# Separate TensorE allowances for preparation and layer 1, and the norm behind layer 1's attention as a thread of its own

## The chip, the cores and the metric

The kernel runs on one core of a Trainium2 chip. The metric is the device time of one execution in microseconds (us); lower is better. Executions of one kernel scatter by about 0.3% here, so kernels are compared by several runs taken on the same chip in the same rounds. The record marks every timed run below as fast (none is over 1.5% above the fastest of the same kernel), so fast runs are compared with fast ones.

## The reference, cut to what matters

Eight images of 256 channels and 32x32 pixels go through two layers in float32. Layer 0 has eight heads that attend from 1024 pixels to 1426 pooled keys. Layer 1 is one full attention over an image's 1024 tokens, followed by eight experts that every token visits.

```python
# layer 0: keys and values from four pooled sizes with a depthwise convolution
attn = softmax(einsum('bhqd,bhkd->bhqk', q_g, k) * SCALE)      # 1024 x 1426 per head
x = x + proj(einsum('bhqk,bhkd->bhqd', attn, v) ...)
# layer 1
t = to_tokens(x)
t = t + attention(_ln_t(t))                                    # 1024 x 1024, one head of 256
t = t + experts(_ln_t(t))                                      # 8 experts, two hidden layers, one output
```

The gates of the experts need the mean over all images, so the last expert products can only start when layer 1's attention is done for the last image. Until then the first two products of some experts are computed and their result is parked in HBM ("staged").

## The kernel before

A scheduler at build time (`Flow`) fixes the order of every engine's instructions. The main loop emits layer 0's attention in 384 steps: four score matmuls, one exponential on ScalarE, four value matmuls of the step before. Between the steps it resumes threads of other work, as long as an allowance of TensorE time lasts. A thread says before each piece on which engine it will run and which tiles it needs.

```python
PACE = 3.2
CAP = 1.5

    def runnable(self, need):
        engine, tiles, tag = need
        ...
        if engine == "PE":
            until = max(pe, self.free("sc") - 0.5)        # when the scores' buffer comes free
            slot = self.free(tag) if tag is not None else 0.0
            return (not self.closed
                and (self.credit > 0 or pe < until - 0.5) # allowance left, or TensorE idle anyway
                and at + MARGIN <= until and slot <= until)
        ...
    def resume(self, thread):
        ...
        self.credit -= self.now["PE"] - pe                # what the piece took
    def step(self, pace=None):
        ...
            self.credit = min(self.credit + pace, CAP * pace)
        while True:
            thread = next((t for t in self.threads if self.runnable(t[1])), None)
```

Threads are kept by rank: queries 0, projection 1, keys and values 2, preparation of the next image 4, layer 1's outputs 5, layer 1's scores 6, the convolution on VectorE 7. The output of layer 1 for one quarter of an image, with its norm inline:

```python
        def outputs():
            for i in range(4 * nb):
                ...
                res = T(l1, [P, 2, C], "res")
                f.sp.dma_start(res, t1[b][:, :, q])
                ...                                        # sums, reciprocal, 16 matmuls into ps
                o = T(l1, [P, 2, C], "o")
                f.ve.tensor_tensor(o, ps, rec, ALU.mult)
                for m in range(2):
                    f.ve.scalar_tensor_tensor(o[:, m, :], o[:, m, :], gb[:, m : m + 1], res[:, m, :], ALU.add, ALU.add)
                f.sp.dma_start(t2[b][:, :, q], o)
                yield from scale_tokens(o, C)              # the norm
                f.sp.dma_start(hn[b][:, :, q], o)
```

Two further places matter below. The projection of layer 0 adds the residual from one tile, `xr`, which is loaded, added to and stored four times for an image. The exponentials are summed in pairs by accumulating transfers, which GpSimd issues in its own program order, between the operations that pool the next image.

```python
    xt = T(work, [P, 512], "xr")
    f.sp.dma_start(xt, x[b, m * P : (m + 1) * P, sl])
    yield pe(atts[b, 0], atts[b, 1], tag="sm")
    ps = small()                                           # matmuls into a small PSUM buffer
    yield ve(ps, xt)
    f.ve.scalar_tensor_tensor(xt, ps, bias[:, m : m + 1], xt, ALU.add, ALU.add)
```

Of the kernel before, what the change touches and what calls it, by code (L numbers as in the profile page):

```python
# [11 lines left out]
ALU = mybir.AluOpType  # L12
# [4 lines left out]
P = 128  # L17
C = 256
HW = 1024
HEADS = 8  # L20
DH = 32
# [4 lines left out]
NE = 8  # L26
SCALE0 = DH ** -0.5
SCALE1 = C ** -0.5
PACE = 3.2
CAP = 1.5  # L30
NEVER = 1e9
MARGIN = 1.5
AHEAD = {"DVE": 4.0, "ACT": 2.0, "POOL": 4.0, "SP": 10.0}
# [2 lines left out]
PACE2 = 8.0  # L36
# [617 lines left out]
class Flow:  # L654
# [18 lines left out]
    def __init__(self, tc, kit):  # L673
        nc = tc.nc
        self.tc, self.kit = tc, kit
        self.now = dict.fromkeys(("PE", "DVE", "ACT", "POOL", "SP"), 0.0)
        self.last = {}
        self.ready, self.read, self.writer, self.reader, self.slots, self.open = {}, {}, {}, {}, {}, set()
        self.pe = self.Engine(self, "PE", nc.tensor)
        self.ve = self.Engine(self, "DVE", nc.vector)  # L680
        self.act = self.Engine(self, "ACT", nc.scalar)
        self.pool = self.Engine(self, "POOL", nc.gpsimd)
        self.sp = self.Engine(self, "SP", nc.sync)
        self.threads = []
        self.cut = {}
        self.also = {}
        self.credit, self.port = 0.0, 0.0

    def tile(self, pool, shape, tag, bufs=1):
        t = self.kit.tile(pool, shape, tag, bufs=bufs)  # L690
# [111 lines left out]
            self.threads.insert(at, thread)  # L802
        return thread

    def runnable(self, need):
        engine, tiles, tag = need
        if engine is None:
            return tiles()
        at = max([self.ready.get(n, 0.0) for t in tiles for n in self.keys(t)], default=0.0)
        pe = self.now["PE"]  # L810
        if engine == "PE":

            until = max(pe, self.free("sc") - 0.5)
            slot = self.free(tag) if tag is not None else 0.0
            return (
                not self.closed
                and (self.credit > 0 or pe < until - 0.5)
                and at + MARGIN <= until
                and slot <= until
            )  # L820

        now = self.now[engine]
        return now <= pe + AHEAD[engine] if at <= now + 0.3 else at <= pe + NEAR[engine]

    def resume(self, thread):
        pe = self.now["PE"]
        thread[1] = next(thread[0], None)
        if thread[1] is None:
            self.threads = [t for t in self.threads if t is not thread]
        self.credit -= self.now["PE"] - pe  # L830

    def step(self, pace=None):


        self.closed = pace is None
        if pace is not None:
            self.credit = min(self.credit + pace, CAP * pace)
        while True:
            thread = next((t for t in self.threads if self.runnable(t[1])), None)
            if thread is None:  # L840
                return
            self.resume(thread)

    def finish(self, done):

        while not done():
            self.credit, self.closed = 1.0, False
            thread = next((t for t in self.threads if t[1][0] is None and self.runnable(t[1])), None)
            self.resume(thread or min((t for t in self.threads if self.possible(t[1])), key=self.start))

# [11 lines left out]
def attention(tc, kit, f, outer, ended, nb, consts, x, t1, t2, hn, bounds, vecs, q_t, kv_t, proj_t, gqk_t, wqk, wqkv, vecs1, w1_d, w1c, gate_d, wrc, vecs2, bnvec):  # L862
# [6 lines left out]
    with ExitStack() as ctx:  # L869
        l1, shared = outer  # L870
# [4 lines left out]
        def T(pool, shape, tag, bufs=1):  # L875
            return f.tile(pool, shape, tag, bufs=bufs)
# [31 lines left out]
        pjw = weight(proj_t, "v", 256, l1)  # L908
        con = kit.con
        ident, grp = kit.ident, con[:, K_GRP : K_GRP + P]  # L910
        heads = T(l1, [P, P + DH], "o")
        nc.scalar.dma_start(heads, consts[:, K_HEAD:K_SEL])
        head = heads[:, :P]

# [692 lines left out]
        def outputs():  # L1607

            for i in range(4 * nb):
                yield until(lambda: len(probabilities) > i)  # L1610
                b, q, p1, v = probabilities[i]
                res = T(l1, [P, 2, C], "res")
                f.sp.dma_start(res, t1[b][:, :, q])
                s = T(l1, [P, 2, C], "s")
                yield ve(*p1[:2])
                f.ve.tensor_tensor(s, p1[0], p1[1], ALU.add)
                for g in range(2, 4):
                    yield ve(p1[g])
                    f.ve.tensor_tensor(s, s, p1[g], ALU.add)
                f.ve.tensor_tensor(s[:, 0, :], s[:, 0, :], s[:, 1, :], ALU.add)  # L1620
                yield pe(s, tag="sm")
                ps = small()
                f.pe.matmul(ps[:, :C], lhsT=kit.ones, rhs=s[:, 0, :], start=True, stop=True)
                yield ve(ps)
                rec = T(l1, [P, C], "rec1")
                n = 8 * (i // 4) + 4 + i % 4
                f.act.activation(ps[:, C:], ps[:, :C], AF.Copy, accum_out=hi[:, n : n + 1])
                f.ve.reciprocal(rec, ps[:, :C])
                f.act.activation(ps[:, C:], rec, AF.Copy, accum_out=lo[:, n : n + 1])
                yield pe(*p1, v, tag="sm")  # L1630
                ps = small()
                for m in range(2):
                    for kc in range(8):
                        if kc % 4 == 0 and (m or kc):
                            yield pe()
                        f.pe.matmul(
                            ps[:, m * C : (m + 1) * C],
                            lhsT=v[:, kc, m * P : (m + 1) * P],
                            rhs=p1[kc // 2][:, kc % 2, :],
                            start=kc == 0,  # L1640
                            stop=kc == 7,
                        )
                taken[0] += 1
                yield ve(ps, rec)
                o = T(l1, [P, 2, C], "o")
                f.ve.tensor_tensor(
                    o, ps.rearrange("p (m q) -> p m q", m=2), rec[:, None, :].to_broadcast([P, 2, C]), ALU.mult
                )
                for m in range(2):
                    f.ve.scalar_tensor_tensor(o[:, m, :], o[:, m, :], gb[:, m : m + 1], res[:, m, :], ALU.add, ALU.add)  # L1650
                f.sp.dma_start(t2[b][:, :, q], o)
                yield from scale_tokens(o, C)
                f.sp.dma_start(hn[b][:, :, q], o)
                written[0] += 1
                ended[0] = written[0] // 4

        def centred(cm, src, width, dst):

# [14 lines left out]
        def weights1():  # L1673
# [15 lines left out]
            ps = small()  # L1689
# [20 lines left out]
            ps = small()  # L1710
# [28 lines left out]
                f.ve.tensor_tensor(c, c, be_, ALU.add)  # L1739

            for e in range(NE):
                we = T(l1, [P, 2, C], "res")
                f.sp.dma_start(we, w1_d[:, e])
                yield act(we)
                wc = T(l1, [P, 2, C], "o")
                yield from centred(cm, we, C, wc)
                f.sp.dma_start(w1c[:, e], wc)
            wr = T(wp, [P, 2, NE], "wr")
# [30 lines left out]
        for i in range(len(steps) + 1):  # L1779
            if i < len(steps):  # L1780
                b, c, half, kc = steps[i]
                sl = slice(half * 512, half * 512 + 512)
                if kc % 4 == 0:
                    f.finish(lambda: key_parts[0] > 3 * b + kc // 4)
                if (half, kc) == (0, 0):
                    f.finish(lambda: (b, c) in qs)
                    turn[0] = 2 * b + c
                    atts[b, c] = T(work, [P, HW], "att", bufs=2)
                pts[i] = scores(b, c, sl, kc)
                f.step()  # L1790
            if i:
                b1, c1, half1, kc1 = steps[i - 1]
                if kc1 == 0:
                    pv = T(psum, [P, 512], "pv")
                    pairs = []
                    sl1 = slice(half1 * 512, half1 * 512 + 512)
                    f.spawn(unit(b1, c1, sl1, i // NKC, pairs), 0)
                f.finish(lambda: kc1 // 4 in vts[b1])
                values(b1, c1, kc1, pts[i - 1], pv)
                if kc1 % 2:  # L1800
                    add(kc1, pts.pop(i - 1), pts[i - 2])
                    pairs.append(pts.pop(i - 2))
                if kc1 == NKC - 1:
                    f.finish(lambda: projected[0] >= b1)
                    f.act.activation(atts[b1, c1][:, sl1], pv, AF.Copy)
            if i < len(steps):
                f.step(PACE)
        f.finish(lambda: projected[0] == nb)
        f.also.clear()
        f.finish(lambda: f.free("sx") < NEVER)  # L1810
# [138 lines left out]
def experts(tc, kit, nb, t2, hn, h2d, w1c, w2_d, wo_d, bnvec, bo_d, gate_d, wrc, consts8, out, f, outer, ended, early):  # L1949
# [11 lines left out]
    with ExitStack() as ctx:  # L1961
# [152 lines left out]
        while not gated and n2 < NSTAGED:  # L2114
            first(n1)
            n1 += 1
            f.step(PACE2)
            if n1 > 1:
                for _ in second(n2, True):
                    pass  # L2120
                n2 += 1
                f.step(PACE2)
        f.finish(lambda: gated)
        early.close()
        wp3 = ctx.enter_context(tc.tile_pool(name="w3", bufs=1, side="right"))
# [309 lines left out]
```

## Time and profile before

| | before |
|---|---|
| time, median of 6 runs (range) | 3496.1 us (3487.3 to 3504.5) |
| profiled span | 3505.2 us |
| TensorE busy | 3237.3 us |
| TensorE idle | 267.9 us, of it 191.2 in layer 0's attention |
| layer 0's attention (first to last exponential) | 106.8 to 2100.7 us |
| first matmul of the experts / first final expert product | 2134.4 / 2405.0 us |

The profile shows for each engine the time in which it had an instruction in work. A matmul that runs at half clock counts as busy, for twice as long: four records of one kind that take 1.88 us elsewhere take 3.78 us behind a gap shown below. This turns out to matter. The prediction below quotes the lines of before; in a line by stretch the columns are the stretch, its length, the busy time of TensorE, its weight loads, VectorE, ScalarE and GpSimd (instructions in brackets), the granted TensorE clock, the DMA share and GB/s.

### The profile page before, as it was taken

What the parts mean: (1) busy time and instruction counts of PE and PEld (TensorE: products, weight loads), DVE (VectorE), ACT (ScalarE), POOL (GpSimd) and SP (SyncE); (2) the same over time, 40 slices, a digit from 0 to 9 for tenths busy, and PEclk for the clock granted to TensorE, in tenths of its full rate; (3) what the DMA queues carried; (4) which work ended last, traced back from release to release, by engine and by line L of the source; (5) the groups of instructions that cost most, each with busy time, mean ns of one, the idle gap of its engine ahead of it and who ended that gap; (6) DMA issues with size and microseconds to landing.
All of it is one profiled execution on the core that took longest, in us unless ns stands there. A gap on an engine that the chain in (4) does not pass through costs nothing.

```text
span 3505.2 us, 39918 instructions
## 1 busy us (share of the span) xinstructions
PE 3237.3 (92%) x15276; PEld 1790.8 (51%) x15276; DVE 2278.6 (65%) x3922; ACT 1676.3 (48%) x2195; POOL 489.1 (14%) x616
## 2 busy tenths in 40 slices
PE   7787899899989989989999997998999999999998
PEld 3322244344424434433544354745777777777776
DVE  6686888778878787685554443314776656666665
ACT  3565766556566565555564542332223333333332
POOL 2122122131131221321121110004000000000000
PEclk9798999999999999999999999999999999999999
DMA  1356655645655564554555556223440000000000
GB/s 47 75 107 152 134 127 111 144 108 111 148 105 110 134 136 109 119 124 111 112 125 136 128 105 219 79 79 107 150 150 19 19 18 24 31 18 19 19 12 20
DMA packets 103880, 333.28 MB, mean 95 GB/s; under 512 B 12848, under 2 KB 38200, under 8 KB 80448
## 3 DMA queue, kind: packets, MB, share of 16 engines
q0 software_dynamic: 24576, 172.51, 25.1%
q1 hardware_dynamic: 75744, 156.16, 13.0%
q8 instruction: 122, 2.00, 0.2%
q10 hardware_dynamic: 3360, 1.97, 0.2%
q14 instruction: 78, 0.64, 0.1%
HBM read 96.23 MB, written 61.87 MB: 45 GB/s over the span
## 4 chain that ended last, share of the span: by engine, by line
PE 53%; DMA 3%; DVE 3%; ACT 2%; issue 1%; POOL 0%; SPq 0%; DVEq 0%; ACTq 0%; POOLq 0%
PE bank L667 24%; PE y L667 11%; PE sm L667 9%; PE sc L667 3%; PE sx L667 3%; PE pv L667 3%; ACT pt L667 2%; DMA pt<-pt 1%; DMA t<-xr 1%; DVE acc L667 1%; DVE rec L667 1%; DMA t<-t 0%; DMA hn<-hn 0%; DMA xr<-in_x_dram 0%; DVE t L667 0%
## 5 line engine op out<-in xcount | busy, mean ns | idle before, releaser
L667 ACT ACTIVATE pt<-sc 128x2048 f32<-128x2048 f32 (+1 forms) x384 | 720.5, 1876 | 358.5 <-PE sc L667 263.0
L667 PE MATMUL sc<-q,kn 32*128 32x512 f32 (+1 forms) x3072 | 460.8, 671 | 134.1 <-ACT pt L667 132.7
L667 DVE SCALAR_TENSOR_TENSOR acc<-p,vec,acc 128x225 f32<-128x225 f32 (+7 forms) x928 | 521.1, 568 | 34.0 <-ACT acc L667 9.3
L667 PE MATMUL bank<-h,w2e 128*128 128x512 f32 x1024 | 481.2, 596 | 0.0
L667 ACT ACTIVATE h<-bank,bnvec 128x512 f32<-128x512 f32 x298 | 229.7, 771 | 480.0 <-PE bank L667 480.0
L667 DVE TENSOR_TENSOR pt<-pt,pt 128x1024 f32<-128x1024 f32 x320 | 383.8, 1242 | 104.7 <-DMA pt<-pt 100.0
L667 PE MATMUL pv<-pt,vt 128*32 128x512 f32 (+1 forms) x3072 | 429.5, 632 | 2.1 <-ACT att L667 2.1
L667 ACT ACTIVATE h<-c,bnvec 128x512 f32<-128x512 f32 x214 | 162.5, 807 | 322.9 <-DVE c L667 322.9
L667 POOL DMA_DIRECT2D pt<-pt x192 | 169.2, 881 | 994.7 <-ACT pt L667 872.4
L667 PEld LDWEIGHTS sc<-q,kn 32*128 32x128 f32 (+1 forms) x3072 | 119.8, 184 | 339.6 <-ACT pt L667 232.4
L667 DVE TENSOR_TENSOR c<-p1c,bank 128x512 f32<-128x512 f32 x107 | 73.6, 688 | 316.9 <-PE bank L667 316.9
L667 PEld LDWEIGHTS bank<-h,w2e 128*128 128x128 f32 x1024 | 194.8, 191 | 151.7 <-issue 139.9
L667 PEld LDWEIGHTS pv<-pt,vt 128*32 128x32 f32 (+1 forms) x3072 | 61.3, 109 | 315.3 <-issue 296.5
L667 POOL TENSOR_TENSOR rstd<-rstd,mhalf 128x4 f32<-128x4 f32 (+2 forms) x88 | 108.8, 1237 | 735.4 <-DVE rstd L667 602.0
L667 DVE TENSOR_TENSOR h<-h,gates 128x1024 f32<-128x1024 f32 x128 | 156.9, 1226 | 71.5 <-DMA h<-h 64.4
L667 PE MATMUL bank<-hn,w1e 128*128 128x256 f32 (+1 forms) x596 | 189.9, 447 | 10.5 <-DMA w2e<-in_w_dram 10.5
L667 PE MATMUL y<-t,s3e 128*128 128x256 f32 x768 | 187.5, 380 | 0.0
L667 PE MATMUL sm<-y,t 128*128 128x256 f32 x736 | 173.2, 383 | 0.0
L667 ACT ACTIVATE p<-sm 128x512 f32<-128x512 f32 (+1 forms) x151 | 88.2, 584 | 169.6 <-PE sm L667 143.5
L667 PEld LDWEIGHTS bank<-hn,w1e 128*128 128x128 f32 x596 | 114.0, 192 | 100.4 <-issue 92.7
L667 DVE RECIPROCAL rec<-rec 128x512 f32<-128x512 f32 x32 | 107.3, 3352 | 89.1 <-ACT rec L667 89.0
L667 PE MATMUL bank<-t,s1e 128*128 128x256 f32 x642 | 156.1, 379 | 2.9 <-DVE t L667 2.9
(291 smaller groups left out, 4679.2 us busy)
## 6 DMA issues: line engine op xcount, KB each, us to landing
pt<-pt POOLq DMA_DIRECT2D x160, 1024.0 KB, 7.4
h<-h SPq DMA_DIRECT2D x72, 512.0 KB, 4.0
xi<-in_x_dram SPq DMA_DIRECT2D x16, 512.0 KB, 7.2
t<-t SPq DMA_DIRECT2D x8, 1024.0 KB, 5.8
res<-t SPq DMA_DIRECT2D x32, 256.0 KB, 6.0
t<-o SPq DMA_DIRECT2D x32, 256.0 KB, 2.8
hn<-o SPq DMA_DIRECT2D x32, 256.0 KB, 5.6
hn<-hn SPq DMA_DIRECT2D x16, 512.0 KB, 5.3
```

The lines of the kernel that those rows point to most:

```text
L667: ins = fn(*args, **kwargs)
```

## The change

The one allowance becomes two. Threads of rank 0 to 4 (the attention's own side work and the next image's preparation) get 4.0 us for each step, threads of rank 5 and up (layer 1) get 2.0 us, each with a carry-over of 1.5 steps. The norm behind layer 1's attention becomes a thread, so that the next quarter's output need not wait for it. To make room, the multiplication by the reciprocal writes PSUM in place, the sum goes into the residual's tile, and that tile gets a second buffer while tile `o` goes.

```diff
-PACE = 3.2
-CAP = 1.5
+FILLER = 5
+PACE = 4.0
+PACE1 = 2.0
+CAP = (1.5, 1.5)
...
-                and (self.credit > 0 or pe < until - 0.5)
+                and (self.credit[rank >= FILLER] > 0 or pe < until - 0.5)
...
-        self.credit -= self.now["PE"] - pe
+        self.credit[thread[2] >= FILLER] -= self.now["PE"] - pe
...
-            self.credit = min(self.credit + pace, CAP * pace)
+            for i in range(2):
+                self.credit[i] = min(self.credit[i] + pace[i], CAP[i] * pace[i])
...
-                res = T(l1, [P, 2, C], "res")
+                yield until(lambda: scaled[0] >= i - 1)
+                res = T(l1, [P, 2, C], "res", bufs=2)
...
-                o = T(l1, [P, 2, C], "o")
-                f.ve.tensor_tensor(o, ps..., rec..., ALU.mult)
+                m2 = ps.rearrange("p (m q) -> p m q", m=2)
+                f.ve.tensor_tensor(m2, m2, rec..., ALU.mult)
                 for m in range(2):
-                    f.ve.scalar_tensor_tensor(o[:, m, :], o[:, m, :], gb..., res[:, m, :], ALU.add, ALU.add)
-                f.sp.dma_start(t2[b][:, :, q], o)
-                yield from scale_tokens(o, C)
-                f.sp.dma_start(hn[b][:, :, q], o)
-                written[0] += 1
+                    f.ve.scalar_tensor_tensor(res[:, m, :], m2[:, m, :], gb..., res[:, m, :], ALU.add, ALU.add)
+                f.sp.dma_start(t2[b][:, :, q], res)
+                f.spawn(norm(b, q, res), 5)
+        def norm(b, q, o):
+            yield from scale_tokens(o, C)
+            f.sp.dma_start(hn[b][:, :, q], o)
+            scaled[0] += 1
+            written[0] += 1
...
-                f.step(PACE)
+                f.step((PACE, PACE1))
```

More of the change, by code (lines that the diff above doesn't have):

```diff
@@ L686, in __init__ @@
         self.also = {}
-        self.credit, self.port = 0.0, 0.0
+        self.credit, self.port = [0.0, 0.0], 0.0
     def tile(self, pool, shape, tag, bufs=1):
@@ L803, in spawn, with runnable @@
         return thread
-    def runnable(self, need):
+    def runnable(self, need, rank=0):
         engine, tiles, tag = need
@@ L836, in step @@
         if pace is not None:
-            self.credit = min(self.credit + pace, CAP * pace)
+            for i in range(2):
+                self.credit[i] = min(self.credit[i] + pace[i], CAP[i] * pace[i])
         while True:
-            thread = next((t for t in self.threads if self.runnable(t[1])), None)
+            thread = next((t for t in self.threads if self.runnable(t[1], t[2])), None)
             if thread is None:
@@ L846, in finish @@
         while not done():
-            self.credit, self.closed = 1.0, False
+            self.credit, self.closed = [1.0, 1.0], False
             thread = next((t for t in self.threads if t[1][0] is None and self.runnable(t[1])), None)
@@ L910, in attention @@
         ident, grp = kit.ident, con[:, K_GRP : K_GRP + P]
-        heads = T(l1, [P, P + DH], "o")
+        heads = T(l1, [P, P + DH], "res", bufs=2)
         nc.scalar.dma_start(heads, consts[:, K_HEAD:K_SEL])
@@ L1644, in outputs @@
                 yield ve(ps, rec)
-                o = T(l1, [P, 2, C], "o")
-                f.ve.tensor_tensor(
-                    o, ps.rearrange("p (m q) -> p m q", m=2), rec[:, None, :].to_broadcast([P, 2, C]), ALU.mult
-                )
+                m2 = ps.rearrange("p (m q) -> p m q", m=2)
+                f.ve.tensor_tensor(m2, m2, rec[:, None, :].to_broadcast([P, 2, C]), ALU.mult)
                 for m in range(2):
-                    f.ve.scalar_tensor_tensor(o[:, m, :], o[:, m, :], gb[:, m : m + 1], res[:, m, :], ALU.add, ALU.add)
-                f.sp.dma_start(t2[b][:, :, q], o)
-                yield from scale_tokens(o, C)
-                f.sp.dma_start(hn[b][:, :, q], o)
-                written[0] += 1
-                ended[0] = written[0] // 4
+                    f.ve.scalar_tensor_tensor(res[:, m, :], m2[:, m, :], gb[:, m : m + 1], res[:, m, :], ALU.add, ALU.add)
+                f.sp.dma_start(t2[b][:, :, q], res)
+                f.spawn(norm(b, q, res), 5)
+        scaled = [0]
+        def norm(b, q, o):
[3 more added lines that the diff above has]
+            written[0] += 1
+            ended[0] = written[0] // 4
         def centred(cm, src, width, dst):
@@ L1741, in weights1 @@
             for e in range(NE):
-                we = T(l1, [P, 2, C], "res")
+                we = T(l1, [P, 2, C], "res", bufs=2)
                 f.sp.dma_start(we, w1_d[:, e])
                 yield act(we)
-                wc = T(l1, [P, 2, C], "o")
+                wc = T(l1, [P, 2, C], "res", bufs=2)
                 yield from centred(cm, we, C, wc)
@@ L2116, in experts @@
             n1 += 1
-            f.step(PACE2)
+            f.step((PACE2, PACE2))
             if n1 > 1:
@@ L2121, in experts @@
                 n2 += 1
-                f.step(PACE2)
+                f.step((PACE2, PACE2))
         f.finish(lambda: gated)
```

## The prediction

> **What bounds the kernel now.** I read the page's slices first, then the busy time of each engine by stretch, then the waits of TensorE, then the instructions in order of time at two places. The slices (tenths busy, 40 slices of 87.6 us):
>
> ```profile
> PE   7787899899989989989999997998999999999998
> DVE  6686888778878787685554443314776656666665
> PEclk9798999999999999999999999999999999999999
> ```
>
> TensorE is at 7 to 9 tenths through slice 24 and nearly full after it; VectorE, at 6 to 8 in the first half, never is. A full TensorE cannot gain from a reordering, so only its idle time counts. The stretches are the four groups of images of layer 0's attention, the start of the tail, the rest of the tail (layer 1 of the last image beside staged expert work), and the experts proper. First column the length, second TensorE busy, the third from the end the granted clock:
>
> ```profile
> 106.80:459.40 352.60, 282.22 (x1595) 101.34 (x1597) 263.50 (x514) 217.45 (x255) 71.71 (x83) 0.90 0.56 124
> 459.40:1032.80 573.40, 523.95 (x2902) 234.56 (x2898) 455.29 (x822) 349.22 (x430) 142.31 (x169) 0.96 0.55 123
> 1032.80:1607.80 575.00, 531.61 (x2926) 243.21 (x2930) 457.64 (x807) 345.89 (x423) 120.04 (x145) 0.97 0.54 120
> 1607.80:2100.70 492.90, 464.94 (x2643) 228.79 (x2637) 255.85 (x397) 268.41 (x297) 71.20 (x82) 0.98 0.54 120
> 2100.70:2200.00 99.30, 79.85 (x248) 43.37 (x247) 38.15 (x60) 23.43 (x38) 7.75 (x8) 0.91 0.60 206
> 2200.00:2404.00 204.00, 197.45 (x616) 111.61 (x614) 39.61 (x79) 74.71 (x117) 14.81 (x31) 0.98 0.21 78
> 2404.00:3505.00 1101.00, 1083.53 (x4156) 790.63 (x4156) 699.36 (x1083) 354.31 (x553) 27.71 (x42) 0.99 0.13 45
> ```
>
> Idle TensorE, length less busy: 70.4 + 49.4 + 43.4 + 28.0 = 191 us in the attention, 19.5 and 6.6 in the tail, 17.5 in the experts. The attention's share of it is what this change can reach. The waits of TensorE in 106 to 2101 us (us in total, times, longest):
>
> ```profile
> PE sc L667 <- ACT pt L667: 132.7, 96, 7.6
> PE sm L667 <- DVE xr L667: 23.7, 6, 5.9
> PE sx L667 <- DMA res<-in_w_dram: 7.3, 1, 7.3
> ```
>
> So 132.7 of the 191 us are scores that wait for the exponential of the step before. Two steps in order of time show the loop:
>
> ```profile
> 1003.16 1.14 PE L667 MATMUL sc<-q,kn 32*128 32x512 f32 x8 [0.65 <-ACT pt L667]
> ...
> 1004.23 1.06 PE L667 MATMUL pv<-pt,vt 128*32 128x512 f32 x8
> ...
> 1004.41 1.88 ACT L667 ACTIVATE pt<-sc 128x2048 f32<-128x2048 f32 x1 [1.31 <-PE sc L667]
> ...
> 1006.35 1.14 PE L667 MATMUL sc<-q,kn 32*128 32x512 f32 x8 [1.05 <-ACT pt L667]
> ```
>
> A step cannot be shorter than 1006.35 - 1003.16 = 3.19 us: scores 1.14, exponential 1.88, handovers. TensorE's own work in it is 1.14 + 1.06 = 2.2 us. So a step with less than 1.0 us of filler (preparation of the next image, or layer 1) leaves TensorE idle, and a step with more is bound by TensorE. That is the lever of this scheduler, and the allowances set how much filler goes into each step.
>
> **What the Trainium skill says.** "PSUM — Partial Sum Buffer", Specifications: 8 banks of 512 FP32 values in each partition. The program takes all eight (scores 4, two small, one spare small, one for the values), so the scores have one buffer; the trace agrees, each score group waiting for the exponential that empties it. "Perfetto Trace Analysis", Identifying Performance Opportunities: repeated gaps can mean too little PSUM for the next tile; here the 96 waits on one tile are that. "TensorE: Matmul & The Clock Gate", Part 2, Step-by-step: matmuls stay in program order. The trace agrees: an expert matmul that waits 10.46 us for its weights (below) holds up layer 1's work behind it. The same page, What's actually happening: after an idle window of about 3.4 us the clock is halved; the trace agrees, since those eight records took 5.92 us, and the next eight of the same kind 3.60.
>
> **The change, part by part.** I compared the instruction order of the two built programs.
>
> *Removed or added work: none on TensorE.* Every kind of matmul has the same count in both (1536 value matmuls, 512 products of layer 1's scores, 512 of its outputs, 84 plain first-layer expert matmuls, so 21 staged expert steps in both). VectorE keeps its three operations per output; the multiplication now writes PSUM in place (0.69 us each before), the two adds read PSUM and write the residual's tile (0.50 us each before). A small PSUM buffer is thus held about 2 x 0.5 = 1 us longer, 32 times, with three such buffers: I put this at nothing.
>
> *Moved work.* I gave each filler matmul its time from the trace (four 128x256 matmuls 1.73 us, four 128x512 3.6 us, a transpose 0.167 us), and added it up between one score group and the next. Before: 550 us of layer 1 and 400 us of the rest inside the attention. Check: 384 x 2.2 = 845, and 845 + 950 = 1795 us, against 282.2 + 524.0 + 531.6 + 464.9 = 1803 us busy in the trace. After: 509 and 400. So 41 us of layer 1 leave the attention for the tail. The reason is the last five half-image units: no preparation is left, the old single allowance of 3.2 went wholly to layer 1, and the new allowance for layer 1 is 2.0.
>
> *Idle time.* Steps with under 1.0 us of filler: 94 before (62 of them empty), beside 96 waits in the trace; 91 after (54 empty). The shortfall below 1.0 us, summed over the steps, is 72.8 us before and 66.5 after. One wait cost 132.7 / 96 = 1.38 us, so 3 to 5 fewer save 4 to 7 us; I take 7. The warm-up (70 us idle) gets nothing: in the first six units there is one image to prepare and no layer 1 yet, and their filler sums are equal within 3 us. The residual tile's waits (23.7 us) are in code that is not touched.
>
> *The tail.* At the end of the attention the new order has more ready layer-1 work (44 score products and 60 output products of the last image but one, against 4 and 16). Only some of it stands ahead of the first expert matmul, and that matmul waits for weights loaded once the attention's memory is free:
>
> ```profile
> 2111.46 3.01 PE L667 MATMUL sx<-pt,con 128*32 128x512 f32 x8 [2.56 <-issue]
> ...
> 2119.38 1.12 PE L667 MATMUL sm<-att,mt 128*128 128x512 f32 x2 [1.83 <-DVE att L667]
> ...
> 2134.40 5.92 PE L667 MATMUL bank<-hn,w1e 128*128 128x512 f32 x8 [10.46 <-DMA w2e<-in_w_dram]
> ```
>
> In the new order four 128x512 matmuls (3.6 us) of layer 1 stand in the small gaps before the projection, so I count 4 us gained; the 10.46 us stay.
>
> *Sum.* Attention 1994 - 41 - 7 = 1946 us, ending near 2053 instead of 2101. Tail 303 + 41 - 4 = 340, ending near 2393 instead of 2404. Experts 1101, unchanged. That is 11 us off the span; from the timed median, 3497 - 11 = 3486 us. By choice I go to 3481: waits other than the floor (some 25 us of the 191, and exponentials late by more than the floor) should shrink a little where the norm no longer holds up the next output.
>
> **The rivals.** (a) *Idle filled better than my step count says.* If the norm's own thread keeps layer 1 always ready, and fillers wait less for their inputs, perhaps a third of the 121 us idle after the warm-up goes: 40 us, time near 3450. For it: the change exists for this, and 60 us of the score waits exceed the 72.8 us of shortfall. Against: the new order has almost as many starved steps. (b) *The probability buffers become the limit.* Steps of 1 to 2 us of filler rise from 59 to 110, and some units fall to about 44 us by my sum, whereas no unit in the trace took under 48 us. ScalarE waited 54.2 us in the attention for the accumulating transfers that free these buffers (7.4 us to landing). That would give back 5 to 15 us: time 3485 to 3500. (c) *The tail does not absorb 41 us.* It holds 21 staged steps in either program, so layer 1 gets denser there; if its chain of small operations starves TensorE, which was full from 2200 to 2380 us, up to 20 us are lost: time near 3505. (d) *VectorE becomes the bound.* It is busy 455 of 573 us in the second stretch; a stretch 2% shorter takes it to 81%, so this is unlikely.
>
> **Range and chances.** Work on TensorE is constant, so the time moves by idle time alone: 191 us in the attention, of which 70 are out of reach. A gain of 2% is 70 us, over half of the other 121: 8%. A loss of 2% would need 70 us of new idle: 2%. Within 2%: 90%. The range runs from rival (a), a little short of its 3450, to rival (c) with a little noise: 3447 to 3508.
>
> **What would show it right or wrong.** In the new profile: the last exponential near 2053 us (not near 2100); TensorE busy about 3237 us as now; score waits on the exponential near 126 us and 91 to 93 times; the hole before the first expert matmul still above 8 us; the switch to the experts proper near 2393 us; 21 staged steps. It is wrong if the score waits fall under 95 us (rival a), if ScalarE's waits on accumulating transfers rise by over 20 us (b), or if TensorE shows new gaps in the tail (c).

## The result, and the profile after

The changed kernel is correct and took 3455.8 us (median of 6 runs, 3450.9 to 3460.7) against 3496.1 us (6 runs) before. The ratio is 0.9887, with a 95% interval from 0.9867 to 0.9907: 1.1% less time. A ratio here is the mean time of one kernel's fast runs over that of the other's of the same rounds, so it is not quite the ratio of the medians.

The slices of the changed kernel, as those of before in the prediction:

```profile
PE   7788889979989899999989989999999999999998
DVE  6686877787888788787654534316776666666665
PEclk9789999999999999999999999999999999999999
```

To the eye little differs: the low slice at the end of the attention is slice 24 with 8 tenths now, and was slice 25 with 7 tenths before. The stretches tell more. First those of before (units 6 to 15 of the attention, units 16 to 31, the hole before the first expert matmul, the tail up to the first final expert product), a unit being 12 steps, or half of the pixels of four heads:

```profile
459.40:1096.70 637.30, 586.78 (x3238) 263.85 (x3230) 514.59 (x907) 391.06 (x484) 147.71 (x178) 0.97 0.54 121
1096.70:2100.70 1004.00, 933.73 (x5233) 442.71 (x5226) 654.19 (x1119) 572.46 (x667) 185.84 (x218) 0.97 0.54 122
2100.70:2134.40 33.70, 17.37 (x60) 7.82 (x58) 15.16 (x23) 3.21 (x8) 2.16 (x3) 0.86 0.42 123
2134.40:2405.00 270.60, 259.96 (x805) 147.21 (x805) 63.48 (x115) 94.92 (x147) 21.40 (x36) 0.97 0.33 120
```

And the same of the changed kernel:

```profile
453.10:1097.00 643.90, 587.18 (x3238) 266.33 (x3238) 516.74 (x904) 389.72 (x483) 146.81 (x178) 0.96 0.54 119
1097.00:2020.80 923.80, 876.04 (x5039) 402.30 (x5032) 635.08 (x1081) 561.75 (x645) 183.70 (x214) 0.99 0.59 130
2020.80:2055.90 35.10, 24.91 (x99) 15.06 (x98) 17.16 (x18) 5.92 (x14) 0.82 (x1) 0.89 0.37 112
2055.90:2351.60 295.70, 287.02 (x950) 172.68 (x950) 80.89 (x155) 101.43 (x163) 21.31 (x30) 0.98 0.33 117
```

Up to unit 16 nothing moved in sum: both kernels are at 1097 us. The second half of the attention became 80 us shorter, with 22.5 us less idle TensorE (70.3 to 47.8) and a clock of 0.99 in place of 0.97. The hole lost 6 us of idle time, and the tail took the work that the attention gave up.

The instruction count of TensorE is the same on both pages, 15276 matmul records, yet its busy time fell from 3237.3 to 3212.7 us. That is the clock. The trace's throttle records list every stretch at half clock: 36 of them before, 26 after, all but one in each about 3.4 us or a multiple. In them TensorE was busy 172.2 us before and 123.2 us after. Half of that is what the half clock cost, 86.1 and 61.6 us, and the difference, 24.5 us, is all of the fall in busy time. So the span is a sum of three terms:

| | before | after | difference |
|---|---|---|---|
| work at full clock (busy less the clock's cost) | 3151.2 | 3151.1 | -0.1 |
| idle TensorE | 267.9 | 239.2 | -28.7 |
| cost of the half clock | 86.1 | 61.6 | -24.5 |
| span | 3505.2 | 3452.0 | -53.2 |

The first row stays within 3151 +- 5 us in 14 of the other 16 profiles of this study that add no work to the experts or nearly none; the two with the most idle time (runs 4 and 8) read 3139 and 3143. The profile of before was one of its slower executions (3505.2 us against a median of 3496.1), so the profiles show 53 us where the medians show 40. It is the only profile of before. With the profile of run 1, the changed kernel again, the differences are -31.8 us of idle time and -18.3 us of half clock.

Idle time also has two kinds. I added up the intervals in the attention in which no matmul was in work, and split them at 2.5 us, a limit chosen by me. (In these two profiles a stretch at half clock starts in, or within 3.4 us after, 32 of the 36 gaps above it, but only 19 of the 121 gaps of 1 to 2.5 us.) The short ones are 100.8 us before and 101.2 us after. The long ones are 21 with 90.4 us before, and 15 with 69.8 us after. All the idle time that the attention lost was in long gaps. Runs 1, 5 and 6 below have the same attention as the changed kernel and show the scatter: short gaps 94.7 to 103.5 us, long ones 68.6 to 73.2 us, and a cost of the half clock in the attention of 51.1 to 55.6 us, where before has 69.9. So the drop in long gaps and in the half clock is clear of it, and a change of a few us in the short gaps would not show. By what ended them: the residual's addition 23.7 to 8.8 us, the exponential 53.4 to 49.9 us, others 13.3 to 11.1 us. Two of the long gaps of before, in order of time, with the wait in brackets (the exponential is shown with its own wait):

```profile
1392.08 3.78 PE L667 MATMUL sm<-xi,qw 128*128 128x512 f32 x4 [5.86 <-DVE xr L667]
...
1575.67 1.88 ACT L667 ACTIVATE pt<-sc 128x2048 f32<-128x2048 f32 x1 [7.50 <-DMA pt<-pt]
...
1577.60 2.09 PE L667 MATMUL sc<-q,kn 32*128 32x512 f32 x8 [6.18 <-ACT pt L667]
```

In the first, a matmul of the preparation waits for a small PSUM buffer, whose reader on VectorE waits for the residual tile's load. The four records after it took 3.78 us, and four such records take 1.9 us at full clock: the gap of 5.86 us cost 1.9 us beyond itself. In the second, the scores wait for an exponential that had itself waited 7.50 us for an accumulating transfer. The waits of TensorE in the attention of the changed kernel:

```profile
PE sc L669 <- ACT pt L669: 123.1, 97, 12.6
PE sm L669 <- DVE xr L669: 10.3, 5, 4.6
```

Score waits are still 97 in number. Their longest, 12.6 us, is new, and its cause can be read from the order of time:

```profile
730.55 3.75 POOL L669 TENSOR_TENSOR pool<-pool,xi 128x320 f32<-128x320 f32 x2
...
736.45 0.96 POOL L669 DMA_DIRECT2D pt<-pt  x1
...
744.22 1.88 ACT L669 ACTIVATE pt<-sc 128x2048 f32<-128x2048 f32 x1 [12.82 <-DMA pt<-pt]
```

GpSimd issues the accumulating transfer of a pair of exponentials only after its pooling operations; it lands late, its buffers come free late, and ScalarE waits 12.8 us for one, with TensorE behind it. The changed kernel has a fault of its own here, which a better order could remove.

The hole before the experts stayed as forecast, with another transfer named:

```profile
2055.90 5.07 PE L669 MATMUL bank<-hn,w1e 128*128 128x512 f32 x8 [10.19 <-DMA hn<-hn]
```

### The profile page after: what moved, and what is told of

Its sections match the earlier page's. It is cut to its first block, busy times and chain, and to the rows that moved or that the text cites. A ratio compares the mean times of both kernels' runs of the same rounds, so it can differ in the third digit from the quotient of the medians.

```text
span 3452.0 us, 39939 instructions
## 1 busy us (share of the span) xinstructions
PE 3212.7 (93%) x15276; PEld 1785.8 (52%) x15276; DVE 2286.3 (66%) x3922; ACT 1673.9 (48%) x2195; POOL 496.1 (14%) x616
## 4 chain that ended last, share of the span: by engine, by line
PE 73%; DVE 10%; DMA 6%; ACT 5%; issue 3%; POOL 2%; ACTq 0%; SPq 0%; POOLq 0%; DVEq 0%
PE bank L669 24%; PE sm L669 17%; PE y L669 11%; PE sc L669 8%; PE sx L669 6%; PE pv L669 6%; ACT pt L669 4%; DVE acc L669 4%; DMA pt<-pt 3%; DVE pt L669 1%; DVE rec L669 1%; DMA hn<-pool 1%; DMA t<-xr 1%; POOL pool L669 1%; DMA xr<-in_x_dram 1%
## 5 line engine op out<-in xcount | busy, mean ns | idle before, releaser
L669 PE MATMUL sc<-q,kn 32*128 32x512 f32 (+1 forms) x3072 | 458.3, 667 | 124.2 <-ACT pt L669 123.1
L669 DVE SCALAR_TENSOR_TENSOR acc<-p,vec,acc 128x225 f32<-128x225 f32 (+7 forms) x928 | 530.4, 578 | 39.6 <-ACT acc L669 14.9
L669 DVE TENSOR_TENSOR pt<-pt,pt 128x1024 f32<-128x1024 f32 x320 | 384.7, 1246 | 85.1 <-DMA pt<-pt 68.4
L669 DVE TENSOR_TENSOR c<-p1c,bank 128x512 f32<-128x512 f32 x107 | 73.5, 687 | 313.7 <-PE bank L669 313.7
L669 DVE TENSOR_TENSOR h<-h,gates 128x1024 f32<-128x1024 f32 x128 | 157.4, 1230 | 66.3 <-DMA h<-h 59.0
L669 PE MATMUL sm<-p,v 128*128 128x256 f32 x800 | 187.0, 385 | 0.5 <-ACT sm L669 0.5
L669 PEld LDWEIGHTS sm<-p,v 128*128 128x128 f32 x800 | 149.8, 191 | 48.3 <-issue 27.7
```

The source lines that it names most:

```text
L669: ins = fn(*args, **kwargs)
```

## The experiments

Eighteen runs were made, and all were correct. Times are medians; "before" in a ratio is the kernel before in the same rounds (its median was 3496 to 3500 us in each). The last four columns are from each run's one profile, in us; idle and half-clock cost are over the span, long gaps (2.5 us and more) in the attention. At a bar of 2%, run 4 is slower, runs 15 and 16 are unclear (their intervals contain 2%), and the others count as the same; every interval but that of run 14 excludes 1. Runs 5 and 6 were executed once each (3643.0 and 3694.4 us, state unknown) and stand apart below. In the recorded expectations a starved step is one with under 1 us of filler, the shortfall is what such steps lack of 1 us, added up over the order, and cold cost is the cost of the half clock.

| run | kernel | median | ratio to before, 95% | idle | half clock | long gaps |
|---|---|---|---|---|---|---|
| - | before | 3496.1 | 1 | 267.9 | 86.1 | 21, 90.4 |
| - | changed | 3455.8 | 0.9887, 0.9867 to 0.9907 | 239.2 | 61.6 | 15, 69.8 |
| 1 | changed, again | 3457.4 | 0.9880, 0.9865 to 0.9895 | 236.1 | 67.8 | 16, 73.2 |
| 2 | thread and tiles only | 3467.8 | 0.9917, 0.9901 to 0.9933 | 247.4 | 62.9 | 17, 73.1 |
| 3 | two allowances only | 3467.0 | 0.9918, 0.9902 to 0.9933 | 242.9 | 72.2 | 19, 76.2 |
| 4 | changed, one shared 6.0 | 3615.6 | 1.0339, 1.0320 to 1.0358 | 369.2 | 102.6 | 28, 114.7 |
| 7 | changed, 3.2 and 2.0 | 3457.5 | 0.9888, 0.9872 to 0.9905 | 227.6 | 75.5 | 17, 73.5 |
| 8 | changed, 4.0 and 3.2 | 3533.7 | 1.0103, 1.0086 to 1.0120 | 308.1 | 82.2 | 20, 94.4 |
| 9 | tiles only | 3467.0 | 0.9905, 0.9887 to 0.9923 | 246.3 | 59.6 | 19, 81.7 |
| 10 | changed, 4.0 and 1.7, carry-over 1.0 | 3480.7 | 0.9952, 0.9935 to 0.9969 | 254.3 | 68.4 | 15, 82.1 |
| 11 | changed, pooling split | 3448.9 | 0.9841, 0.9821 to 0.9861 | 227.1 | 67.6 | 15, 60.5 |
| 12 | changed, projection held back | 3448.0 | 0.9850, 0.9831 to 0.9870 | 232.3 | 61.1 | 13, 54.2 |
| 13 | before at 3.0 | 3477.9 | 0.9944, 0.9925 to 0.9962 | 248.7 | 66.2 | 18, 85.3 |
| 14 | before at 3.4 | 3503.6 | 1.0012, 0.9999 to 1.0025 | 290.1 | 68.6 | 23, 114.9 |
| 15 | 11 and 12 together | 3434.2 | 0.9813, 0.9787 to 0.9838 | 224.7 | 59.5 | 11, 50.7 |
| 16 | 15 with 3.2 and 2.0 | 3421.2 | 0.9781, 0.9757 to 0.9805 | 208.5 | 57.8 | 9, 37.4 |
| 17 | tiles only at 3.0 | 3482.0 | 0.9958, 0.9945 to 0.9971 | 254.5 | 73.5 | 19, 97.2 |
| 18 | tiles only at 3.4 | 3484.3 | 0.9962, 0.9949 to 0.9975 | 265.8 | 68.0 | 18, 86.0 |

Two profiles of the changed kernel (the second and third rows) differ by 3 us of idle time and by 6 us of half-clock cost. So a single profile's split is good to about that, and part of the scatter between executions can be the clock.

### Runs 1 to 4: the parts

Run 1 is the changed kernel again. Run 2 keeps the thread and the tiles and gives every thread the old single allowance:

```diff
-FILLER = 5
-PACE = 4.0
+FILLER = 99
+PACE = 3.2
```

Run 3 is the kernel before with the diff's allowance lines alone. Run 4 is run 2 with `PACE = 6.0`.

> The changed kernel once more, as the measure for the other runs of this call: every theory expects 0.985 to 0.992 of before (about 3456 us), a granted clock near 0.972, some 123 us of score waits on the exponential in the attention.

> The norm's own thread and the tiles of the change, but the old single allowance of 3.2. Theory A (the two allowances make the gain, by spacing the filler): 3485 to 3498 us, clock near 0.966, score waits near 130 us; the order has 91 steps under 1 us of filler and 66.0 us of shortfall, as the changed kernel has, so a pure count of starved steps would expect the changed kernel's time. Theory B (the norm's thread makes it, by keeping layer 1 ready): 3453 to 3465 us. If both add: near 3475.

> The two allowances of 4.0 and 2.0, but the norm inline behind the output and the old tiles. Theory A: 3453 to 3466 us, clock 0.970 or more. Theory B: 3490 us or more (the order has 100 starved steps and 72.9 us of shortfall, as before has). If both add: near 3475. 24 staged expert steps in place of 21 cost about 1 us.

> The norm's thread with one shared allowance of 6.0, the sum of the two. Theory C (the larger sum of the allowances is what helps, not that they are apart): 3450 to 3470 us. Theory A: slower than before, 3520 us or more, since the preparation and layer 1 then run out early in each image and the order has 179 starved steps with 146.9 us of shortfall: at least 74 us more idle than before, and more by the clock.

Each half gains some 30 us alone, and both together 41 us: neither theory A nor B, and not their sum. Run 4 kills theory C: a larger sum of allowances, shared, makes the kernel 3.4% slower, as theory A said. Its waits of scores on exponentials:

```profile
PE sc L669 <- ACT pt L669: 233.2, 183, 7.7
```

183 waits in place of 97. Work that is let in early is missing later, so a step is left without filler.

### Runs 5 and 6: what a gap costs

To measure the clock by itself I put pauses into the experts of the changed kernel, where TensorE is otherwise busy all the time. A probe matmul reads a tile, GpSimd writes the tile, a second probe reads it. Run 5 has a short pause in every turn of the loop, run 6 a long one in every fourth.

```diff
+        def probe():
+            f.pe.matmul(bank()[:, :8], lhsT=stall[:, :P], rhs=stall[:, :8], start=True, stop=True)
+        def pause():
+            turns[0] += 1
+            if turns[0] % EVERY == 0:                       # 1, or 4
+                probe()
+                for _ in range(TIMES):                      # 1, or 4
+                    f.pool.tensor_tensor(stall[:, :WIDTH], stall[:, :WIDTH], stall[:, :WIDTH], ALU.add)   # 256, or 512
+                probe()
         while n3 < total:
+            pause()
```

> The changed kernel with 114 short pauses of TensorE put into the experts, where it is otherwise busy: a probe matmul, one GpSimd addition of 128x256 on the tile that it read, and a probe that reads the result. Estimated pause 1.2 to 1.8 us, 140 to 200 us of new idle in all. Theory D (idle stretches of several us cost more than themselves, because the clock is halved after them): the span grows by the new idle and little more, the cost of the half clock in the experts stays under 8 us. Rival E (every us of idle costs one us, the clock follows the share of busy time): cold cost grows as much here as in the next run.

> The same with 28 long pauses, each four GpSimd additions of 128x512: an estimated 5 to 6 us each, 140 to 170 us of new idle in all. Theory D: the span grows by the new idle and 45 to 100 us more, as TensorE's busy time for the same work, since each pause halves the clock for one or two stretches of 3.4 us. Rival E: the span grows by the new idle alone, or by the same surplus as with the short pauses.

These two were looked at once, without timed rounds and in an unknown state, so only what the profile shows of the experts is used. One pause of each, in order of time, first the short kind:

```profile
2510.84 0.39 PE L669 MATMUL bank<-stall 128*128 128x8 f32 x2 [0.81 <-POOL stall L669]
2511.09 1.96 PE L669 MATMUL bank<-h,w2e 128*128 128x512 f32 x4
```

then the long kind:

```profile
2513.96 0.60 PE L669 MATMUL bank<-stall 128*128 128x8 f32 x2 [5.84 <-POOL stall L669]
2514.41 3.42 PE L669 MATMUL bank<-h,w2e 128*128 128x512 f32 x4
```

The four records behind the short pause took 1.96 us, those behind the long one 3.42 us. The experts as a whole, from the first to the last final product, short pauses:

```profile
2386.30:3627.10 1240.80, 1151.32 (x4595) 848.56 (x4595) 686.60 (x1066) 366.27 (x553) 67.38 (x110) 1.00 0.11 39
```

and long ones:

```profile
2352.40:3678.60 1326.20, 1166.12 (x4262) 838.89 (x4262) 763.42 (x1075) 357.23 (x553) 182.23 (x163) 0.92 0.11 37
```

The changed kernel's experts are 1086.0 us long with 1083.4 us busy. The 111 short pauses added 86.8 us of idle time (1240.80 - 1151.32, less the 2.7 us that was there) and 68 us of busy time, 0.61 us for each pair of probes; the clock stayed at 1.00. The 27 long pauses added 157.4 us of idle time and 82.7 us of busy time. Their probes explain 27 x 0.61 = 16.5 us of it; the other 66 us, 2.5 us for each pause, are the half clock, and the granted clock fell to 0.92. So a pause of 0.8 us costs itself, and one of 5.8 us costs itself and 2.5 us more. The trace's own half-clock records in these stretches say the same: a cost of 2.0 us in the changed kernel, 3.0 with the short pauses and 69.4 with the long ones. Theory D holds, rival E does not: at 87 of 157 us of idle time it would want over half of the long pauses' surplus with the short ones, and got 1 us. The idle totals came out unequal (87 and 157 us) because the short pauses were shorter than my estimate; per us of idle the surplus is 0.42 us for the long pauses and, by the unchanged clock, about none for the short.

The Trainium skill, "TensorE: Matmul & The Clock Gate", HAM oscillation — how this bites in real kernels, works the penalty out as the throttled time x (1 - 1.2/2.4), that is half of it. With the trace's stretches at half clock as the throttled time, the whole of before would give 239.9 us x 0.5 = 120 us; the profile shows 86, because TensorE was idle for part of that time, and idle time at half clock costs nothing further.

### Runs 7 and 8: which allowance

```diff
 run 7: -PACE = 4.0    +PACE = 3.2
 run 8: -PACE1 = 2.0   +PACE1 = 3.2
```

> The changed kernel with allowances of 3.2 and 2.0 in place of 4.0 and 2.0: only layer 1's own, smaller allowance and the norm's thread are left of the change. Its order has 75 steps under 1 us of filler and 56.1 us of shortfall (changed kernel: 91 and 66.5). Theory F (it is the shortfall that counts, at some 1.8 us of time for each us of it, as between the norm-only and the shared-6.0 kernels): 3435 to 3445 us. Theory G (the larger allowance for the preparation is needed): 3457 us or more.

> The changed kernel with allowances of 4.0 and 3.2: apart, but layer 1's as large as the old shared one. The order has 130 starved steps and 110.5 us of shortfall. Theory F: 3457 + 44 x 1.8 = 3536 us, at least 3515. If keeping the two apart were what helps: 3450 to 3470 us.

Run 8 came out within 3 us of the forecast: with layer 1's allowance at 3.2 the changed kernel is slower than before. So the separation alone does not help; layer 1's own allowance must also be held down. Only 3.2 and 2.0 were compared with all else equal, and smaller is not always better: run 10, with 1.7 and a smaller carry-over, is slower again. Run 7 equals the changed kernel: raising the preparation's allowance to 4.0 contributes nothing that shows. Its forecast from the shortfall, 3435 to 3445 us, was missed, although idle time fell by 12 us in its profile; the half clock took as much back (61.6 to 75.5 us, one profile each).

### Runs 9 to 12: tiles, evenness, and two sources of long gaps

```diff
 run 9 (on run 2): -f.spawn(norm(b, q, res), 5)               +yield from norm(b, q, res)
 run 10:           -PACE1 = 2.0, CAP = (1.5, 1.5)             +PACE1 = 1.7, CAP = (1.5, 1.0)
 run 11:           +yield pool(xi) between the pooling operations of GpSimd, 7 places
 run 12:           -yield pe(atts[b, 0], atts[b, 1], tag="sm") +yield pe(atts[b, 0], atts[b, 1], xt, tag="sm")
```

> The tiles of the change (two residual buffers, the multiplication in place in PSUM) with the norm inline behind the output again, and the single allowance of 3.2. It differs from the norm-only kernel (3468 us) by the thread alone, and from before by the tiles alone. If the thread makes the norm part's gain of 30 us: 3490 to 3505 us (its order has 97 starved steps and 77.0 us of shortfall, against 94 and 72.8 of before). If the tiles make it: 3465 to 3475 us.

> The changed kernel with layer 1's allowance at 1.7 and its carry-over at 1.0: the most even filler of 36 orders looked at (76 starved steps, 52.7 us of shortfall, 161 steps of 1 to 2 us), but 28 staged expert steps in place of 21, which cost 7 x 0.43 = 3 us. If shortfall is what sets the time (1.7 us of idle for each us of it, the clock's cost with it): 3457 - 14 x 1.7 + 3 = 3436 us or less. If the profit is used up, as with 3.2 and 2.0: 3452 to 3462 us.

> The changed kernel with a scheduling point between GpSimd's pooling operations, so that the accumulating transfers of the probabilities, which GpSimd issues, need not wait behind up to seven of them. If late issues make the longest gap (12.6 us at 734 us in the changed kernel): that gap goes, gaps of 2.5 us and more fall from 70 to 55 us, 3435 to 3450 us. If not: 3452 to 3462 us.

> The changed kernel with the projection's matmul held back until the residual's tile is taken to be loaded, so that a small PSUM buffer is not held while VectorE waits for that load. If these waits can be had so: waits of TensorE on the residual's addition fall from 12.9 us to under 5, 3445 to 3452 us. Against: the order's shortfall rises from 66.5 to 69.0 us, and the model's latency for the load is 3.0 us where the trace shows up to 8.6; then 3455 to 3470 us.

Run 9 takes the thread out of run 2 and loses nothing (3467.0 against 3467.8 us). So under the old allowance no gain of the thread, after which the change is partly named, can be seen. Run 10 was a clear miss: the order with the smallest shortfall is 23 us slower than the changed kernel. Its long gaps hold 82.1 us, its full-clock work is 5 us more, and idle time is 15 us more. The shortfall orders kernels when it differs by 40 us and more (runs 4 and 8), and fails when it differs by 10 to 14 (runs 7 and 10). Runs 11 and 12 went at long gaps that the profile had named. Both gained about 9 us over run 1 by their medians (10 to 14 us by the ratios to before). In run 12 no long gap waits for the residual's addition any more; in run 11 the 12.6 us gap is gone. That the named gaps went is shown; that their going made the 9 us is not, by the measure of the next two runs.

### Runs 13 and 14: how far the order alone moves the time

```diff
 run 13: -PACE = 3.2   +PACE = 3.0
 run 14: -PACE = 3.2   +PACE = 3.4
```

> The kernel before with its single allowance at 3.0 in place of 3.2, nothing else. Theory H (the order's chance placing of long gaps moves the time by 20 to 40 us, whatever is changed): 3460 to 3485 us or 3510 us and more. Theory I (the parts of the change have their gains for themselves, and a small step of the old allowance is nearly neutral): 3490 to 3505 us. Shortfall 66.3 us (before 72.8).

> The kernel before with its single allowance at 3.4. Theory H: off by 15 us or more from before in either direction. Theory I: 3490 to 3510 us. Shortfall 81.1 us, so a pure count would say 3497 + 8 x 1.8 = 3512 us.

The kernel before at 3.0, 3.2 and 3.4 takes 3478, 3496 and 3504 us. Run 13 is as theory H said, run 14 as theory I said: 7 us off, where H wanted 15. These three alone would also fit a trend, since their shortfall (66.3, 72.8, 81.1 us) rises with the time. Against a trend stand the kernels with the change's tiles at the same constants, 3482, 3467 and 3484 us (runs 17, 9 and 18). Either way one constant, moved by 6%, is worth 18.5 us, nearly half of the change's whole gain. So an effect of one part below some 20 us cannot be credited here to that part.

### Runs 15 and 16: fewer long gaps

Run 15 joins the edits of runs 11 and 12; run 16 adds `PACE = 3.2`.

> The changed kernel with both the scheduling points between GpSimd's pooling operations (3449 us alone) and the projection held back for its residual tile (3448 us alone). If long gaps removed add up: 3436 to 3444 us, long gaps under 50 us in the attention. If each was only another order: 3445 to 3460 us.

> As the last, with allowances of 3.2 and 2.0. The 3.2 was neutral in the changed kernel (3457.5 against 3457.4 us), so 3436 to 3450 us if neutral here; a scatter between the two of over 10 us would speak for chance placing of gaps.

Both beat both kernels. Run 15 came out just below what adding the two gains forecast (3434.2 us for 3436 to 3444, long gaps 50.7 us for under 50), run 16 some 15 us below the lower end of its forecast. Run 16 takes 3421.2 us (3418.7 to 3421.7, five runs), 2.2% under before and about 1% under the changed kernel. Its waits on the exponential are still close to a hundred:

```profile
PE sc L669 <- ACT pt L669: 113.6, 94, 7.7
```

Against the changed kernel, short gaps in the attention are 96.4 us (101.2), long ones 9 with 37.4 us (15 with 69.8), three of 5.8 to 7.7 us in the warm-up. That run 16 is 13 us better than run 15, where 7 showed no effect of the same constant, is again the size of the scatter between orders.

### Runs 17 and 18: the tiles at the neighbours

```diff
 on run 9: -PACE = 3.2   +PACE = 3.0 (run 17), 3.4 (run 18)
```

> The tiles of the change, norm inline, one allowance of 3.0 (pair: the kernel before at 3.0, 3478 us). If the tiles gain by themselves: 3440 to 3462 us. If it was chance at 3.2: 3468 to 3490 us.

> The tiles of the change, norm inline, one allowance of 3.4 (pair: the kernel before at 3.4, 3504 us). If the tiles gain by themselves: 3465 to 3488 us. If it was chance at 3.2: 3494 to 3515 us.

Three pairs now differ by the tiles alone: 3478 to 3482, 3500 to 3467 (before in the rounds of run 9), and 3504 to 3484 us. That is +4, -33 and -19 us: run 17 came out as chance forecast, run 18 as a gain of the tiles forecast. A gain of the tiles as such is neither shown nor excluded; their value in the change stays open. So does the value of the thread together with the two allowances: run 3, which has neither thread nor tiles, is 10 us behind run 1, less than the scatter between orders.

## Why the prediction was right or wrong

The direction and the bound were right: TensorE bounds the kernel, its work is the same, and less idle time makes it faster. The size was not: 16 us forecast, 40 us measured, inside the range but 2.5 times the forecast.

**"41 us of layer 1 leave the attention for the tail": right.** Without idle time and the clock's cost the attention holds 40 us less, and the tail 40.5 us more. The check beside it was luck, though: it put a sum of 1795 us against 1803 us busy, but 70 of these 1803 us are the half clock, and the work at full clock is 1733 us. The sum was about 62 us too large, and overlap of the records that it added is of that size (eight records of 3.60 us are followed by the next group after 3.44 us). The two errors nearly cancelled, and the clock stayed out of sight.

**"Work on TensorE is constant, so the time moves by idle time alone" and "TensorE busy about 3237 us as now": this step failed.** Work was constant, busy time was not. The prediction quoted the half clock from the Trainium skill and showed it in two lines, but gave it no term in the sum. It was worth 24.5 us of the 53 between the two profiles: 18.8 in the attention, 6 at its end and in the tail (18.3 us with the profile of run 1). Runs 5 and 6 show that long gaps cause such a cost and short ones do not.

**"One wait cost 1.38 us, so 3 to 5 fewer save 4 to 7 us": the term was mis-sized, because it priced the wrong gaps.** The average mixed short starved steps with rare long gaps: 12 of the 96 waits hold 53.3 of the 132.7 us, and the other 84 cost 0.94 us each. So the prediction's reading that all 96 mean too little PSUM is too simple: in a long one, as at 1577 us above, the exponential itself came late, behind a transfer. Attention idle fell by 20 us, all of it in gaps of 2.5 us and more. The short gaps did nearly as forecast, which is nothing: 101 us in both. (The floor of 3.19 us for a step was read off one pair; the shortest steps of before take 3.04 us.)

**"The residual tile's waits are in code that is not touched": failed.** They fell from 26.6 to 12.9 us (both small buffers taken together; the prediction's 23.7 us are the larger part, which fell to 10.3). The code is untouched, but what stands behind it on TensorE, and needs the small PSUM buffer that it holds, was moved.

**"The hole stays, 4 us gained before it": right in kind.** The wait was 10.19 us after 10.46. Idle time in the hole fell by 6 us and in the rest of the tail by 2.

**Signs that were named.** Score waits near 126 us: 123.1, right, though 97 in number and not 91 to 93. Last exponential near 2053 us: 2020.8. Switch to the experts near 2393 us: 2351.6. 21 staged steps: right.

**The rivals.** Rival (a), with 3450 us, was nearest in time. But its sign, score waits under 95 us, did not come, and its reason found no support: run 9 shows no effect of the thread under the old allowance. Rival (b) did not show on the whole: ScalarE's waits on accumulating transfers went from 56.9 to 60.1 us. One of them, 12.8 us, is the longest gap after. Rivals (c) and (d) did not show: the tail's idle time fell, and VectorE did not bound.

**What is shown and what is not.** It is shown that beside 4.0 an allowance of 3.2 for layer 1 is 76 us slower than one of 2.0 (run 8), that the sum of the two, shared, harms (run 4), and that long gaps cost more than themselves (run 6). The lesser number and cost of long gaps in the changed kernel is measured. That it belongs to the design of the change, and not in good part to the luck of one order, is not shown: the kernel before at 3.0 already gets 18.5 of the 40 us. In its profile the attention from unit 16 on, where the changed kernel lost its 22.5 us, has 46.0 us of idle time and 12.4 us in long gaps, as the changed kernel has (47.8 and 12.1), without any part of the change.

## What to carry to other kernels

Where a TensorE-bound kernel's order is fixed at build time, split its idle time by the length of the gaps and add the half clock as a term of its own: the three add up to the span by definition, and work at full clock stayed within 5 us in nearly every version here, so the other two carried the differences. Then remove long gaps by name, from the order of time; two small repairs and one changed constant gained nearly as much again (3457 to 3421 us) as the whole change, though 13 us of it came with a constant that was neutral elsewhere. Before crediting a part of a scheduling change with a gain of 0.5%, move a neutral constant and see how far that alone goes.

## What the Trainium skill lacked or had wrong

- "TensorE: Matmul & The Clock Gate", HAM oscillation: the penalty as throttled time x (1 - 1.2/2.4) counts idle time too, if the throttled time is the length of the stretches at half clock (the profile metric that the page uses is not in these profiles). Here it would give 120 us for the kernel before; half of the busy time at half clock, 86 us, closes the account.
- The same section gives the rule to avoid gaps above some 3.4 us, and an example in which each gap is followed by 1.67 us of throttled time. Here, inside a stream that is otherwise full, each of 27 gaps of 5.8 us cost 2.5 us beyond itself (the example's 1.67 us at half clock would cost 0.83), and each of 111 gaps of 0.8 us nothing. What lies between was not measured with pauses.
- "Perfetto Trace Analysis", Identifying the Most-Contended Engine, warns of matmul busy time for another reason, pipelining. It does not say that busy time also contains the half clock's cost; the page on TensorE has longer times for a cold matmul, but does not draw this from them: 3237.3 and 3212.7 us for the same 15276 records.
